# Three mixtures of experts in a perceiver network: gates by tiles, prefix sums by doubling, first gathers ahead of the second weights, statistics by four tiles, and the rounding of a layer's weights in cross attention

## The chip, the core and the metric

The kernel runs on one core of a Trainium2 chip. A core has TensorE (PE, with its weight loads as PEld), VectorE (DVE), ScalarE (ACT), GpSimd (POOL) and SyncE (SP); each takes its instructions in the order in which the program has them. The metric is the device time of one execution in microseconds (us); lower is better. Times are medians of several runs, and one further execution is recorded by the profiler.

## The reference, cut to what matters

1024 tokens of 256 numbers (16 batches of 64) go through four layers. Each layer adds to x a cross attention over a context of 1601 rows a batch, a self attention and a feed-forward part, each on a plain layer norm of x. The feed-forward parts of layers 0, 2 and 3 are mixtures of eight experts; layer 1's has two matrices whose weights are rounded to −1, 0, 1 times a scale:

```python
x = x + _L0_ffn_ref(_layernorm(x, axis=-1), L0_ffn_Wg, L0_ffn_W1, L0_ffn_W2, L0_ffn_W3)
...
# a mixture with two choices, layer 3; layer 0 has no capacity and a gated hidden layer
logits = x_flat @ router_w.T
top_v, top_i = jax.lax.top_k(jax.nn.softmax(logits, axis=-1), K)
top_v = top_v / jnp.sum(top_v, axis=-1, keepdims=True)
for k in range(K):
    pos = jnp.take_along_axis(jnp.cumsum(onehot, axis=0), eid[:, None], axis=1)[:, 0] - 1
    keep = pos < C
    ...
    h = jax.nn.gelu(jnp.einsum('ech,ehf->ecf', expert_in, w1), approximate=False)
    y = jnp.einsum('ecf,efh->ech', h, w2)
    out = out + tok * (gate * keep.astype(x.dtype))[:, None]
# layer 2: one choice, logits through a reduction to 16
logits = (x @ wg_red.T) @ wg_unit.T
```

All of it is float32. The kernel need not compute every expert for every token: it sorts tokens by expert.

## The kernel before, in words

x and its normalised copy xn lie on chip, as eight tiles of 128 tokens (NT = 8). The stages follow each other in order: layer 0's cross attention, attention, feed-forward, then layer 1's, and so on. Their times in the profiled execution, from the start of the span: layer 0's mixture 616 to 853, layer 1's cross attention 853 to 1700, its attention 1700 to 1780, its feed-forward 1780 to 1866, layer 2's mixture 2438 to 2595, layer 3's 3051 to 3273.

**A mixture** runs so. `ready` (L298) and `normalise` (L314) make xn of a tile: statistics on DVE, three small operations on POOL with the power −1/2 among them, and one ACT pass. `expert_rows` (L1580) writes xn to DRAM as one transfer (xin, the table that is gathered from) with 128 zero rows behind it, and transposes xn whole. `gate_logits` (L1423) makes the eight logits of each token, 32 matmul records in all; layer 2 goes through 16 numbers first. `top2` and `first_max` (L1405, L1388) find the choices as one-hot tiles on DVE. `places` (L1431) finds each choice's place in its expert's list: a matmul with ones gives counts by tile, one add after the other sums them up over the 16 (layer 2: 8) groups, a matmul with a triangle counts inside a tile. `slots` (L1449) turns places into a row of a tile (lo) and a tile (hi), builds V on DVE and POOL, and for each group compares a row of numbers with lo (R, 128x128) and multiplies R by V; the sums are `token` and `share` for each row of each tile. `rows` holds the expert of each tile and is ready earlier.

`experts` (L1519) then runs 23 tiles (layer 2: 15) of 128 gathered tokens. `fetch` (L1527) reads the expert's row number into a register of SP, starts the tile's weights as two transfers (W, three buffers; 1536 and 768 KB in layer 0, 1024 and 1024 in layer 3, 1024 and 1028 in layer 2) and has POOL gather the rows (xs, three buffers). PE turns xs, makes the hidden layer and the output; DVE scales it by share, and POOL adds it into a DRAM table, `total`, by an indirect transfer. Fetches run two tiles ahead. At the end x is read back in four transfers, and `ready` runs over all tiles.

```python
got = [fetch(0), fetch(1)]
xT = turn(got[0][1])
for i in range(tiles):
    W, xs = got.pop(0)
    if i + 2 < tiles:
        got.append(fetch(i + 2))
```

**Cross attention of layer 1** (L582) has 16 batches of 13 key tiles. At step t PE makes the scores of tile t (pss, two banks), ACT copies them, DVE keeps a running maximum (top); when a batch is over, `turn` (L652) transposes the maximum, DVE reduces it (nm) and makes a diagonal of it (diag), PE spreads it, and `lower` (L670) and `values` (L676) follow 14 and 16 steps behind the scores. The context's tiles come through two ring slots, ctxT (two buffers) and ctx; further weights come through the slots wst. `quant_weight` (L1754) rounds a weight matrix: a DVE reduce of 128x2048, a small matmul, one ACT and two DVE passes. It runs for w1 in this loop (batch 12), and for w2 in layer 1's attention (L1233), step n = 3; w2 is loaded into the wst slot at 1700.90. `add_bias` (L353) adds an output bias to x on POOL, tile by tile.

What sets the order: the program's order inside stretches that are marked fixed and for instructions that are pinned (L193); elsewhere a scheduler may interleave instructions of an engine. Engines wait for each other by semaphores.

Of the kernel before, what the change touches and what calls it, by code (L numbers as in the profile page):

```python
# [16 lines left out]
P = 128  # L17
# [159 lines left out]
class Net:  # L177
    def __init__(self, tc, io):
        self.tc, self.nc, self.io = tc, tc.nc, io
        self.flip = 0  # L180
        self.w1, self.quant_next, self.xscale = None, 0, {}
        self.fixed = False
# [36 lines left out]
    def load_constants(self, pool):  # L219
# [24 lines left out]
        self.ident = self.c("ident")  # L244
        self.due = None
# [67 lines left out]

    def normalise(self):  # L314
# [38 lines left out]
    def add_bias(self, i):  # L353

        for t in range(NT):
            self.nc.gpsimd.tensor_tensor(self.x[:, t, :], self.x[:, t, :], self.bv(i), ALU.add)  # L356
# [225 lines left out]
    def L1_xattn(self, w):  # L582
# [8 lines left out]
        with (  # L591
# [4 lines left out]
            with (  # L596
# [4 lines left out]
                self.add_bias(2)  # L601
# [6 lines left out]
            with (  # L608
# [125 lines left out]

                for b in range(B):
# [14 lines left out]
                if self.w1 is not None:  # L750
                    at(NKT * 12 + 9, self.quant_weight, pst, self.w1, "pst")
                fetch(0)
# [480 lines left out]
    def L1_attn(self, w):  # L1233
# [6 lines left out]
        with tc.tile_pool(name="l1a", bufs=1) as wk:  # L1240
# [32 lines left out]
            with (  # L1273
# [39 lines left out]
                for n in range(NT + 3):  # L1313
# [8 lines left out]
                    if "L1_ffn" in self.held:  # L1322
                        if n == 3:
                            self.quant_weight(psa, self.held["L1_ffn"][1], "py")
# [63 lines left out]
    def first_max(self, small, lg, tag):  # L1388
# [3 lines left out]
        m = small.tile([P, NT, 1], F32, tag=f"m{tag}", name=f"m{tag}")  # L1392
        nc.vector.tensor_reduce(m, lg, AX.X, ALU.max)
        oh = small.tile(shape, F32, tag=f"oh{tag}", name=f"oh{tag}")
# [5 lines left out]
        lo = small.tile([P, NT, 1], F32, tag=f"lo{tag}", name=f"lo{tag}")  # L1400
        nc.vector.tensor_reduce(lo, oh, AX.X, ALU.min)
        nc.vector.tensor_tensor(oh, oh, lo.to_broadcast(shape), ALU.is_equal)
        return m, oh

    def top2(self, small, lg):  # L1405

        nc = self.nc
        shape = [P, NT, E]
        m1, oh1 = self.first_max(small, lg, "a")
        lg2 = small.tile(shape, F32, tag="lg2", name="lg2")  # L1410
        nc.vector.scalar_tensor_tensor(lg2, oh1, -BIG, lg, ALU.mult, ALU.add)
        m2, oh2 = self.first_max(small, lg2, "b")
        e2 = small.tile([P, NT, 1], F32, tag="e2", name="e2")
        nc.vector.tensor_tensor(e2, m2, m1, ALU.subtract)
        nc.scalar.activation(e2, e2, AF.Exp)
        g1 = small.tile([P, NT, 1], F32, tag="g1", name="g1")
        nc.vector.tensor_scalar(g1, e2, 1.0, None, ALU.add)
        nc.vector.reciprocal(g1, g1)
        g2 = small.tile([P, NT, 1], F32, tag="g2", name="g2")
        nc.vector.tensor_tensor(g2, e2, g1, ALU.mult)  # L1420
        return oh1, g1, oh2, g2

    def gate_logits(self, small, pp, xT, w):  # L1423
        ps = self.psum(pp, [P, NT, E], "pst")
        for t in range(NT):
            self.project_N(ps[:, t, :], xT, t, w)
        lg = small.tile([P, NT, E], F32, tag="lg", name="lg")
# [935 lines left out]
```

## Time and profile before

| | us |
|---|---|
| median of 3 runs | 3266.31 |
| lowest, highest run | 3265.10, 3282.47 |
| profiled execution | 3275.31 |
| its span, first to last instruction | 3273.5 |
| granted clock of TensorE, mean | 0.953 |

The page of the profile gives busy times by engine, the span in 40 slices, DMA queues, the chain that ended last, and the costliest groups of instructions. Busy shares of the span: PE 92%, ACT 42%, DVE 39%, POOL 11%; the DMA engines moved 395 MB, 121 GB/s on the mean. Views of single stretches show each instruction as start, duration, engine, line, operation, output and inputs, and in brackets how long its engine was idle before it and what ended that. A view of windows gives the busy time of each engine, the granted clock, the DMA share and the rate in a stretch. Periods of an expert tile, from the same trace: 8.17 in layer 0, 7.24 in layer 2, 7.25 in layer 3.

### The profile page before, as it was taken

Reading aid. Unit: us, or ns where it says so; the run is one execution under the profiler, and the core shown is the slowest. Engines: PE = TensorE matmul, PEld = TensorE weight load, DVE = VectorE, ACT = ScalarE, POOL = GpSimd, SP = SyncE. Lnnn points to the kernel's source line nnn. Section 1 sums busy time; section 2 is a strip of 40 time slices with the busy share of each in tenths; the row PEclk is TensorE's granted clock in tenths of the full one; section 3 lists DMA queues with packets and bytes.
Section 4 is the critical chain, followed back from the end, with each engine's and each line's share of the span. In section 5 each row is a group of like instructions: output and inputs, shape, how many; then the busy total and the mean of one; then the engine's idle time right before and its main releaser. Section 6 shows DMA issues by size and latency. Waiting matters only on the chain. (4 is left out here: it accounts for less than half of the span.)

```text
span 3273.5 us, 67440 instructions
## 1 busy us (share of the span) xinstructions
PE 3021.5 (92%) x28567; PEld 2263.0 (69%) x28567; DVE 1261.0 (39%) x3415; ACT 1362.1 (42%) x2699; POOL 371.6 (11%) x538
## 2 busy tenths in 40 slices
PE   7999997699799999999998999999979798889798
PEld 5666664599556666666666777777748676778697
DVE  6888884422244444444446521221242100035200
ACT  5888884211233333333333522222222387763111
POOL 0000001233200000000010000000012311111232
PEclk9999998699899999999997999999988899999799
DMA  6334431389211121211257011111208555510497
GB/s 216 106 130 134 134 108 42 134 287 323 63 61 61 61 81 44 78 61 61 81 174 221 28 46 55 61 41 61 77 17 300 161 180 187 175 56 1 152 328 241
DMA packets 178362, 395.09 MB, mean 121 GB/s; under 512 B 11446, under 2 KB 142270, under 8 KB 165214
## 3 DMA queue, kind: packets, MB, share of 16 engines
q1 hardware_dynamic: 165070, 372.91, 33.0%
q0 software_dynamic: 11712, 16.00, 2.4%
q8 instruction: 225, 3.69, 0.5%
q10 hardware_dynamic: 1280, 1.88, 0.2%
q14 instruction: 75, 0.61, 0.1%
HBM read 375.02 MB, written 16.12 MB: 119 GB/s over the span
## 5 line engine op out<-in xcount | busy, mean ns | idle before, releaser
L199 PE MATMUL acc<-ctx,st 128*128 128x257 f32 (+1 forms) x1664 | 397.2, 383 | 0.0
L199 PE MATMUL pss<-qk,ctxT 128*128 128x512 f32 (+1 forms) x832 | 388.8, 592 | 0.6 <-DVE qk L634 0.6
L199 PEld LDWEIGHTS acc<-ctx,st 128*128 128x128 f32 (+1 forms) x1664 | 310.1, 190 | 94.6 <-issue 35.6
L459 DVE CUSTOM_DVE_ANT_0 Sx<-s,mneg 128x384 f32<-128x384 f32 (+1 forms) x512 | 264.2, 570 | 88.6 <-PE s L199 88.6
L650 DVE TENSOR_TENSOR top<-pss,top 128x512 f32<-128x512 f32 x192 | 132.7, 691 | 402.4 <-ACT st L645 402.3
L203 PE MATMUL pst<-cst,Sx 128*128 128x128 f32 (+1 forms) x1736 | 255.8, 286 | 25.5 <-ACT Sx L1369 10.3
L674 ACT ACTIVATE st<-st 128x512 f32<-128x512 f32 (+1 forms) x208 | 130.6, 629 | 292.5 <-DVE st L673 292.5
L935 ACT ACTIVATE Pr<-pss 128x512 f32<-128x512 f32 (+1 forms) x512 | 219.9, 523 | 62.1 <-PE pss L199 60.7
L503 ACT ACTIVATE PT<-pst 128x384 f32<-128x384 f32 x512 | 215.1, 489 | 63.4 <-PE pst L203 62.3
L203 PEld LDWEIGHTS pst<-cst,Sx 128*128 128x128 f32 (+1 forms) x1736 | 188.7, 143 | 73.1 <-ACT PT L503 27.8
L199 PEld LDWEIGHTS pss<-qk,ctxT 128*128 128x128 f32 (+1 forms) x832 | 154.1, 186 | 120.7 <-issue 102.7
L645 ACT COPY st<-pss 128x512 f32<-128x512 f32 (+1 forms) x208 | 121.8, 585 | 201.5 <-PE pss L199 201.5
L199 PE MATMUL pso<-W,hT 128*128 128x256 f32 x884 | 200.9, 379 | 0.0
L199 PE MATMUL pst<-wst,ctxT 128*128 128x256 f32 (+1 forms) x832 | 183.4, 380 | 0.0
L199 PE MATMUL psk<-ctxT,wst 128*128 128x512 f32 (+1 forms) x512 | 181.8, 513 | 0.8 <-ACT qT L797 0.8
L199 PEld LDWEIGHTS pso<-W,hT 128*128 128x128 f32 x884 | 163.2, 190 | 19.7
L199 PEld LDWEIGHTS pst<-wst,ctxT 128*128 128x128 f32 (+1 forms) x832 | 153.5, 186 | 25.9 <-issue 2.7
L199 PE MATMUL pss<-q,ctxT 32*128 32x128 f32 (+1 forms) x3328 | 149.6, 298 | 13.6 <-issue 9.5
L199 PEld LDWEIGHTS psk<-ctxT,wst 128*128 128x128 f32 x512 | 88.3, 190 | 93.7 <-issue 92.1
L356 POOL TENSOR_TENSOR x<-x,bvec 128x256 f32<-128x256 f32 x40 | 29.8, 746 | 1079.2 <-ACT xn L317 1079.2
L837 DVE TENSOR_TENSOR v<-pst,bvec 128x512 f32<-128x512 f32 (+1 forms) x112 | 73.1, 653 | 204.4 <-PE pst L199 204.4
L478 ACT ACTIVATE Sx<-Sx,neg 128x384 f32<-128x384 f32 (+1 forms) x256 | 145.8, 620 | 11.5 <-DVE neg L469 11.3
(394 smaller groups left out, 4479.5 us busy)
## 6 DMA issues: line engine op xcount, KB each, us to landing
ctxT<-in_ctxT_dram SPq DMA_DIRECT2D x64, 1601.0 KB
W<-in_L_experts_dram SPq DMA_DIRECT2D x61, 1024.0 KB
ctx<-in_ctx_dram SPq DMA_DIRECT2D x32, 1536.0 KB
W<-in_L_experts_dram SPq DMA_DIRECT2D x23, 1536.0 KB
ctx<-in_ctx_ones_dram SPq DMA_DIRECT2D x16, 1632.0 KB
ctx<-in_ctx_one_dram SPq DMA_DIRECT2D x16, 1542.0 KB
W<-in_L_experts_dram SPq DMA_DIRECT2D x23, 768.0 KB
W<-in_L_experts_dram SPq DMA_DIRECT2D x15, 1028.0 KB
```

The costliest lines, as they stand in the source:

```text
L199: self.pinned(self.nc.tensor.matmul(out, lhsT, rhs, start=start, stop=stop))
L203: self.pinned(self.nc.tensor.transpose(out, in_, self.ident[:n, :n]))
L356: self.nc.gpsimd.tensor_tensor(self.x[:, t, :], self.x[:, t, :], self.bv(i), ALU.add)
L459: self.pinned(nc.vector.tensor_tensor_reduce(out=Sx[:, j, :n], in0=ps[j][:, :n], in1=st["mneg"][:, o : o + n], op0=ALU.add, op1=ALU.max, s ...
L478: self.pinned(nc.scalar.activation(Sj[j], Sj[j], AF.Identity, bias=st["neg"][:, j - 2 : j - 1]))
L503: self.pinned(nc.scalar.activation(PT, ps, AF.Exp))
L645: pin(nc.scalar.copy(st[:kn], ps[:kn]))
L650: pin(nc.vector.tensor_tensor(top[b][:kn], ps[:kn], top[b][:kn], ALU.max))
L674: pin(nc.scalar.activation(st, st, AF.Exp, scale=HD**-0.5))
L837: nc.vector.tensor_tensor(o, ps[:kn, :n, :], bv[:kn].to_broadcast([kn, n, D]), ALU.add)
L935: nc.scalar.activation(st["Pr"][:kn, g : g + n, j, :], ps[j][:kn, :n, :], AF.Silu)
```

## The change

1. **Gates by tiles.** `expert_rows` and the old `gate_logits` go. The new `gate_logits` writes xin tile by tile (eight transfers), turns a tile with two transposes, copies it on ACT, and makes its logits with two matmuls (in layer 2 two more steps: 16 numbers, then logits); turns run one tile ahead. All of it is pinned, and two PSUM buffers serve it. The normalisation of the last tile is pinned after the fourth turn. The zero rows come from one small tile that is filled once at the start.
2. **Choices and prefix sums.** `top2` writes into the joint tiles, without the copies in `two_choices`. `places` copies the counts once and adds them to themselves shifted by 1, 2, 4 and 8 groups.
3. **R four groups wide**: 4 compares of 128x512 in place of 16 of 128x128.
4. **First gathers.** W[0] is fetched, then two gathers are started, and then POOL copies `rows` to `rest`, from which the register for W[1] and all later ones is read.
5. **Statistics by four tiles** (`ready_all`) behind the mixtures of layers 0 and 2: one power on POOL for four tiles, ACT and DVE share the normalising. The bias add of layer 1's cross attention moves from its projections to step 3 of its loop, and bias adds are pinned everywhere.
6. **w2 of layer 1** is loaded into a ctxT slot in cross attention (batch 15, step 1) and rounded there (step 7), no longer in attention. Layer 2's cross attention weights are thereby loaded earlier into wst. The last normalisation before a mixture or layer 1's feed-forward part moves into that part.

```diff
+    def ready_all(self):
+        nc, pin = self.nc, self.pinned
+        self.fixed = True
+        parts = []
+        for h in range(2):
+            mv = self.stat.tile([P, 4, 2], F32, tag="mv4", name="mv4", bufs=2)
+            for i in range(4):
+                st = self.stat.tile([P, 6], F32, tag="bst", name="bst")
+                pin(nc.vector.bn_stats(st, self.x[:, 4 * h + i, :]))
+                pin(nc.vector.bn_aggr(mv[:, i, :], st))
+            rs = self.stat.tile([P, 2, 4], F32, tag="rs4", name="rs4", bufs=2)
+            pin(nc.vector.tensor_scalar(rs[:, 0], mv[:, :, 1], 1e-5, None, ALU.add))
+            nc.gpsimd.tensor_tensor(
+                rs[:, 0], rs[:, 0], self.c("pow")[:, 0:1].to_broadcast([P, 4]), ALU.pow
+            )
+            parts.append((mv, rs))
+        for h, (mv, rs) in enumerate(parts):
+            pin(nc.vector.scalar_tensor_tensor(
+                rs[:, 1], mv[:, :, 0], -1.0, rs[:, 0], ALU.mult, ALU.mult
+            ))
+            for i in range(4):
+                o, x = self.xn[:, 4 * h + i, :], self.x[:, 4 * h + i, :]
+                if i % 2:
+                    pin(nc.vector.tensor_scalar(
+                        o, x, mv[:, i, 0:1], rs[:, 0, i : i + 1], ALU.subtract, ALU.mult
+                    ))
+                else:
+                    pin(nc.scalar.activation(
+                        o, x, AF.Identity, bias=rs[:, 1, i : i + 1], scale=rs[:, 0, i : i + 1]
+                    ))
+        self.fixed = False
...
-            self.nc.gpsimd.tensor_tensor(self.x[:, t, :], self.x[:, t, :], self.bv(i), ALU.add)
+            self.pinned(self.nc.gpsimd.tensor_tensor(
+                self.x[:, t, :], self.x[:, t, :], self.bv(i), ALU.add
+            ))
...
-                self.add_bias(2)
...
+                at(3, self.add_bias, 2)
...
+                    at(NKT * 15 + 1, self.load_w2)
+                    at(NKT * 15 + 7, lambda: self.quant_weight(pst, self.w2, "pst"))
...
-                        if n == 3:
-                            self.quant_weight(psa, self.held["L1_ffn"][1], "py")
...
-        cum = small.tile([P, G + 1, E], F32, tag="cum", name="cum")
-        nc.vector.memset(cum[:, 0, :], 0.0)
-        for g in range(G):
-            nc.vector.tensor_tensor(cum[:, g + 1, :], cum[:, g, :], ps[:, g, :], ALU.add)
-        ps = self.psum(pp, [P, G, E], "pst")
-        self.mm(ps.rearrange("p g e -> p (g e)"), self.c("tri"), flat)
+        within = self.psum(pp, [P, G, E], "pst")
+        self.mm(within.rearrange("p g e -> p (g e)"), self.c("tri"), flat)
+        cum = [small.tile([P, pad + G, E], F32, tag=f"cum{i}", name="cum") for i in range(2)]
+        for c in cum:
+            nc.vector.memset(c[:, :pad, :], 0.0)
+        nc.vector.tensor_copy(cum[0][:, pad:, :], ps)
+        step = 1
+        while step < G:
+            nc.vector.tensor_tensor(
+                cum[1][:, pad:, :], cum[0][:, pad:, :], cum[0][:, pad - step : pad - step + G, :],
+                ALU.add,
+            )
+            cum.reverse()
+            step *= 2
         place = small.tile([P, G, E], F32, tag="place", name="place")
-        nc.vector.tensor_tensor(place, ps, cum[:, :G, :], ALU.add)
-        return place, cum[:, NT, :], cum[:, G, :]
+        nc.vector.tensor_tensor(place, within, cum[0][:, pad - 1 : pad - 1 + G, :], ALU.add)
+        return place, cum[0][:, pad + NT - 1, :], cum[0][:, pad + G - 1, :]
...
-        for g in range(G):
-            R = small.tile([P, P], F32, tag="R", name="R", bufs=3)
-            nc.vector.tensor_scalar(R, self.c("iota128"), lo[:, g : g + 1], None, ALU.is_equal)
-            self.mm(ps, R, V[:, :, g, :], g == 0, g == G - 1)
+        for g in range(0, G, 4):
+            R = small.tile([P, 4, P], F32, tag="R", name="R", bufs=2)
+            nc.vector.tensor_tensor(
+                R, self.c("iota128").unsqueeze(1).to_broadcast([P, 4, P]),
+                lo[:, g : g + 4].unsqueeze(2).to_broadcast([P, 4, P]), ALU.is_equal,
+            )
+            for i in range(4):
+                self.mm(ps, R[:, i, :], V[:, :, g + i, :], g + i == 0, g + i == G - 1)
...
-        def fetch(i):
+        def fetch(i, rows):
             W = wp.tile([P, width], F32, tag="W", name="W", bufs=3)
             r = nc.values_load(
                 rows[0:1, i : i + 1], [mybir.EngineType.SP], min_val=0, max_val=(E - 1) * P
             )
             for o in (slice(0, cols), slice(cols, width)):
                 nc.sync.dma_start(W[:, o], self.io[weights][bass.ds(r, P), o])
+            return W
+        def gather(i):
             xs = sp.tile([P, D], F32, tag="xs", name="xs", bufs=3)
             nc.gpsimd.indirect_dma_start(
                 xs, None, xin, bass.IndirectOffsetOnAxis(token[:, i : i + 1], 0),
                 bounds_check=NTOK + SPARE - 1,
             )
-            return W, xs
+            return xs
...
-        got = [fetch(0), fetch(1)]
-        xT = turn(got[0][1])
+        W, xs = {0: fetch(0, rows)}, [gather(0), gather(1)]
+        rest = sp.tile([P, tiles], U32, tag="rest", name="rest", bufs=1)
+        self.pinned(nc.gpsimd.tensor_copy(rest, rows))
+        W[1] = fetch(1, rest)
+        xT = turn(xs.pop(0))
         for i in range(tiles):
-            W, xs = got.pop(0)
             if i + 2 < tiles:
-                got.append(fetch(i + 2))
-            hT = hidden(W, xT)
+                W[i + 2] = fetch(i + 2, rest)
+                xs.append(gather(i + 2))
+            hT = hidden(W[i], xT)
             if i + 1 < tiles:
-                xT = turn(got[0][1])
+                xT = turn(xs.pop(0))
             n = hT.shape[1]
-            W2 = W[:, cols : cols + n * D].rearrange("p (c n) -> p c n", n=D)
+            W2 = W.pop(i)[:, cols : cols + n * D].rearrange("p (c n) -> p c n", n=D)
...
-            for t in range(NT):
-                self.ready(t)
-    def expert_rows(self, wk, stat, pst, name):
+            self.ready_all()
...
+    def gate_logits(self, name, small, pst):
+        nc, pin = self.nc, self.pinned
+        xin = self.dram.tile([NTOK + SPARE, D], F32, tag=f"{name}i", name=f"{name}i")
+        nc.sync.dma_start(
+            xin[NTOK:, :].rearrange("p (a d) -> p a d", d=64),
+            self.zero.unsqueeze(1).to_broadcast([P, D // 64, 64]),
+        )
+        lg = small.tile([P, NT, E], F32, tag="lg", name="lg")
+        self.fixed = True
+        if name == "l2":
+            sq = small.tile([E, 16], F32, tag="sq", name="sq")
+            nc.vector.tensor_tensor(sq, self.wg2, self.wg2, ALU.mult)
+            nr = small.tile([E, 1], F32, tag="nr", name="nr")
+            nc.vector.tensor_reduce(nr, sq, AX.X, ALU.add)
+            nc.gpsimd.tensor_tensor(nr, nr, self.c("pow")[:E, 1:2], ALU.pow)
+            nc.vector.tensor_scalar(nr, nr, 1e-4, None, ALU.max)
+            nc.vector.reciprocal(nr, nr)
+            wu = small.tile([E, 16], F32, tag="wu", name="wu")
+            nc.vector.tensor_scalar(wu, self.wg2, nr, None, ALU.mult)
+            ps = self.psum(pst, [P, E], "pst")
+            self.tr(ps[:16, :], wu)
+            wuT = small.tile([16, E], F32, tag="wuT", name="wuT")
+            nc.vector.tensor_copy(wuT, ps[:16, :])
+        turned = {}
+        def turn(t):
+            nc.sync.dma_start(xin[t * P : (t + 1) * P, :], self.xn[:, t, :])
+            ps = self.psum(pst, [P, 2, P], "pst")
+            for kc in range(2):
+                self.tr(ps[:, kc, :], self.xn[:, t, kc * P : (kc + 1) * P])
+            turned[t] = small.tile([P, 2, P], F32, tag="gx", name="gx", bufs=2)
+            pin(nc.scalar.copy(turned[t], ps))
+        def logits(t):
+            xT = turned.pop(t)
+            ps = self.psum(pst, [P, P], "pst")
+            if name == "l2":
+                w = self.gates[:, :, 2 * E : 2 * E + 16]
+                for kc in range(2):
+                    self.mm(ps[:16, :], w[:, kc, :], xT[:, kc, :], kc == 0, kc == 1)
+                xr = small.tile([16, P], F32, tag="xr", name="xr", bufs=2)
+                pin(nc.vector.tensor_copy(xr, ps[:16, :]))
+                turned[t] = xr
+                return
+            o = 0 if name == "l0" else E
+            for kc in range(2):
+                self.mm(ps[:, :E], xT[:, kc, :], self.gates[:, kc, o : o + E], kc == 0, kc == 1)
+            pin(nc.vector.tensor_copy(lg[:, t, :], ps[:, :E]))
+        def reduced(t):
+            if name == "l2":
+                ps = self.psum(pst, [P, P], "pst")
+                self.mm(ps[:, :E], turned.pop(t), wuT)
+                pin(nc.vector.tensor_copy(lg[:, t, :], ps[:, :E]))
+        for t in range(NT + 2):
+            if t < NT:
+                turn(t)
+            if 0 <= t - 1 < NT:
+                logits(t - 1)
+            if 0 <= t - 2 < NT:
+                reduced(t - 2)
+            if t == 3:
+                self.normalise()
+        self.fixed = False
+        return xin, lg
...
-        oh = small.tile([P, 2 * NT, E], F32, tag="oh", name="oh")
-        nc.vector.tensor_copy(oh[:, :NT, :], oh1)
-        nc.vector.tensor_copy(oh[:, NT:, :], oh2)
-        gate = small.tile([P, 2 * NT], F32, tag="gate", name="gate")
-        nc.vector.tensor_copy(gate[:, :NT], g1[:, :, 0])
-        nc.vector.tensor_copy(gate[:, NT:], g2[:, :, 0])
...
+    def load_w2(self):
+        (self.w2,) = self.slot(self.stream, "ctxT", (self.io["L1_w2T"],))
...
             turn_x(0)
+            self.normalise()
...
+                after = stages[i + 1] if i + 1 < len(stages) else None
+                load(after)
                 getattr(self, name)(held.pop(name))
-                self.normalise()
+                if after not in ("L0_ffn", "L1_ffn", "L2_ffn", "L3_ffn"):
+                    self.normalise()
```

## The prediction, made before the changed kernel ran

> **What bounds the kernel now.** I read the page first, its share and clock rows, then the costliest groups, and then the stages one by one by the windows and the timeline.
>
> The page's first part:
>
> ```profile
> span 3273.5 us, 67440 instructions
> ## 1 busy us (share of the span) xinstructions
> PE 3021.5 (92%) x28567; PEld 2263.0 (69%) x28567; DVE 1261.0 (39%) x3415; ACT 1362.1 (42%) x2699; POOL 371.6 (11%) x538
> ```
>
> TensorE is busy 92% of the span, and the change takes hardly a matmul out of the long loops. So nothing can be won in cross attention or among the expert tiles: the windows of the loops show PE busy 90.00 of 90.00 us (740 to 830, layer 0) and 80.00 of 80.00 (3100 to 3180, layer 3). What can be won is the 8% in which PE waits, and the change works where much of it sits: ahead of each mixture, and behind two of them. The timeline of layer 0's start (start, duration, engine, line, operation, idle before and who ended it):
>
> ```profile
> 626.79 0.23 DVE L1428 COPY lg<-pst 128x64 f32<-128x64 f32 x1 [5.84 <-PE pst L199]
> 631.03 3.10 DVE L1442 TENSOR_TENSOR cum<-cum,pst 128x8 f32<-128x8 f32 x16 [0.66 <-PE pst L199]
> ...
> 637.70 4.30 SPq L1533 DMA_DIRECT2D W<-in_L_experts_dram  x6
> ...
> 642.75 5.39 PE L199 MATMUL pst<-V,R 128*128 128x69 f32 x24 [1.49 <-DVE R L1506]
> ...
> 649.17 1.30 POOL L1535 DMA_INDIRECT xs<-l0i,token  x1 [9.93 <-DMA W<-in_L_experts_dram]
> ...
> 655.86 0.66 PE L203 MATMUL pst<-cst,xs 128*128 128x128 f32 x2 [7.71 <-DMA xs<-l0i,token]
> ```
>
> One serial chain runs from the logits (626.79) to the first gathered rows (655.86): 29 us with little of PE in it. Its two long links are the prefix sums (3.10 us) and the gather, issued at 649.17 while the six weight DMAs of 637.70 still land; PE waits for it until 655.86, 6.7 us.
>
> **The change, part by part** (us; negative is faster; bounds in brackets).
>
> *1. Gates by tiles.* The windows ahead of the logits (length, PE, PEld, DVE, ACT, POOL, clock, DMA share, GB/s):
>
> ```profile
> 616.00:618.00 2.00, 0.58 (x5) 0.45 (x5) 1.54 (x4) 1.07 (x2) 0.65 (x4) 1.00 0.43 41
> 618.00:620.00 2.00, 0.65 (x6) 0.39 (x4) 0.00 (x0) 0.60 (x1) 0.92 (x3) 1.00 0.89 343
> 620.00:622.00 2.00, 1.44 (x13) 1.22 (x11) 0.69 (x1) 0.59 (x1) 0.00 (x0) 0.99 0.87 293
> 622.00:624.00 2.00, 2.00 (x11) 2.00 (x11) 0.00 (x0) 0.00 (x0) 0.00 (x0) 0.50 1.03 345
> ```
>
> 32 gate matmuls take 5.97 us, mostly at clock 0.50. In their place come eight steps of two transposes, an ACT copy, two matmuls and a small DVE copy. With two PSUM buffers a step is the round trip transposes, copy, next: at full clock 0.28 (eight transposes took 1.09 at 3051.41) + 0.37 (the 128x256 copy of 656.56) + two hand-overs of about 0.1 = 0.87; at half clock 0.69 (the pair of 2598.01) + 0.37 + 0.2 = 1.3. The order of the changed kernel puts every gate transpose behind the last matmul of the stage before, so the steps start near 617.0 in layer 0 and 3051.4 in layer 3. I take five steps at full and three at half clock, 8.2, and 0.6 for the last logits: 625.8 against 626.79, **−1.0** [−2.4, +1.4]; 3060.2 against 3061.75, **−1.5** [−2.8, +0.9]. Layer 2 has three matmul steps a tile, and its first ACT copy stands behind xn6 (done 2442.43): 8 × 1.25 + 1.5 gives 2453.9 against 2452.35, **+1.5** [−1, +4.4]. With no gate transposes between its steps, layer 0's attention loses a stall of 0.8 near 602 (PE waited 2.08 for xn): **−0.8** [−0.8, 0].
>
> [...] The rows show 1.00 from 616 to 620 with PE busy 0.58 and 0.65 of 2 us, and 0.50 only later. [...]
>
> *2. Prefix sums, copies.* 16 dependent adds (3.10) become one PSUM copy (0.28, as the 128x128 add of 634.05) and four adds of 128x128 at 0.32: 1.56, so −1.5; the oh copies save 0.4 on the chain. **−2.0** [−2.2, −1.5] in layers 0 and 3; in layer 2 eight adds (1.55) become one copy and three adds of half the width: **−0.6** [−0.8, 0].
>
> *3. Four-wide R.* 16 compares become four of 128x512 (0.69, the diag product L659). PE's matmuls behind them set the pace (32 in 7.10 us in layer 3), so the compares are hidden, and only the first is 0.41 longer. In layer 0 the 2.28 us reduce of layer 1's weight, which stopped PE 1.49 at 642.75, now stands in DVE's order ahead of the token chain's hi: +2.28 − 1.7. **+0.6** [−0.5, +2.3] and **+0.3** [0, +0.5].
>
> *4. Gathers ahead.* Only W[0] (2.3 MB) lies ahead of the gathers, and at the 380 to 469 GB/s that the DMA view shows from 640 to 652 it has landed some 7 us after 637.70, before they are issued. Over the whole trace a gather lands 2.7 us (shortest) to 4.9 (median) after issue; the first here took 6.7. I take 3.5: **−3.2** [−4, 0], and **−3.1** in layer 3 (its wait is 7.62). Layer 2's first transposes are behind the b2 matmuls (7.27 us from 2465.88), which cover the gather: 0. The added wait: W[1] waits for two gather issues and a POOL copy, about 3.3 us after the first issue, and W[2] is queued behind it on SP. In layer 0 the first half (1.5 MB, about 4.6 us) lands some 6.5 after SP issues it, near 656, needed one tile (about 8 us) after the first hidden matmul, near 658: hidden beside the first tile.
>
> *5. Statistics by four.* POOL's order sets the pace of the transition behind layer 0:
>
> ```profile
> 866.27 2.10 POOL L356 TENSOR_TENSOR x<-x,bvec 128x256 f32<-128x256 f32 x3
> 866.35 0.60 ACT L317 ACTIVATE xn<-x,rs 128x256 f32<-128x256 f32 x1 [1.10 <-POOL rs L311]
> ...
> 867.70 14.74 PE L199 MATMUL pst<-xnT,wst 128*128 128x512 f32 x30
> ```
>
> Statistics reach DVE at 853.48, yet xn7 comes at 866.35, since each tile takes three POOL operations and a bias add, 1.8 us. Now DVE's statistics (0.55 a tile, 8.2 in all with two pow of about 1.0 and four normalisings) give xn7 near 861.7; the projections, 32 × 0.49 behind the last transposes near 862.7, end at 878.4 instead of 882.4: **−4.0** [−5, −2]. Behind layer 2 there were no bias adds (xn7 at 2604.85): **−2.5** [−5, −1]. The adds go into cross attention, where POOL is idle.
>
> *6. Layer 1's w2.* In attention its rounding held DVE from 1751.98 to 1754.54, and PE waited 2.92 for A at 1755.72: **−3.0** [−3, −1]. In cross attention w1's rounding at 1500.4 to 1505.3 stopped PE nowhere. But w2 goes into the slot whose batch ends at 1612.3, and its reduce is in DVE's order between nm and diag of that turn:
>
> ```profile
> 1612.32 0.37 SPq L261 DMA_DIRECT2D ctxT<-in_ctxT_dram  x1
> ...
> 1617.06 0.68 DVE L657 TENSOR_REDUCE nm<-pst 128x4 f32<-128x512 f32 x1
> ...
> 1617.77 0.69 DVE L659 TENSOR_TENSOR diag<-cst,nm 128x512 f32<-128x512 f32 x1
> ```
>
> 1 MB issued at 1612.32 lands near 1618 (the 1.6 MB there now stopped at 1618.2); the reduce (2.29) ends at 1620.3, and behind it on DVE wait diag, the lowering and the next maximum. PE's matmul of diag, at 1619.47 now, comes near 1621.3 or later: **+2.3** [0, +6; the same load took 8.85 at 1700.90]. Layer 1's ffn starts with its normalising after the first transposes, not before its copy: **−1.4** [−1.4, 0]. Earlier weight loads and the zero rows are far ahead of their use: 0.
>
> **Sum.** Layer 0: −0.8 −1.0 −2.0 +0.6 −3.2 = −6.4. Layer 3: −1.5 −2.0 +0.3 −3.1 = −6.3. Layer 2: +1.5 −0.6 = +0.9. Transitions: −6.5. Layer 1: +2.3 −3.0 −1.4 = −2.1. Together **−20.4**. The profiled execution took 3275.31 (span 3273.5, 1.8 outside it); it would take 3254.9. It lay 9.0 above the median 3266.31 and above two of the three runs; the stages summed here are short and serial, so I carry the difference, not a ratio: 3266.3 − 20.4 = **3246**. Errors of separate terms partly cancel: the forecast's own range is 3239 to 3253.
>
> **Rivals.**
> - *Half clock in the gate loops.* All steps at 1.3, layer 2's at 1.6: 2.4 more in layers 0 and 3 each, 2.9 in layer 2, so −12.7: 3254. For it: the clock was 0.50 in 2443 to 2448. Against: the rows above.
> - *The gathers stay slow*, because their time is their own and not the weights': −6.3 is gone, 3252. For it: the longest landing in the trace is 8.1 without such a burst. Against: the median is 4.9 with DMA engines 0.93 to 0.96 busy.
> - *It does not do what it says*: compares and prefix sums hidden, gathers slow, statistics bound by the read of x: only −2.1 of layer 1 and about −3 stay: 3261.
> - *Slower: the weight stream.* The loops move 320 to 335 GB/s with the DMA engines 0.93 to 0.96 busy, and the weights alone need 2.36 MB in 8.17 us, 289 GB/s. The two early weight tiles were a lead, and the change takes it. If W then got under 289 GB/s, each of the 61 tiles would wait: a tile costs 2.36/p or 2.1/p. At p = 260 that is 0.91 × 23 + 0.82 × 23 + 0.82 × 15 = +52, net +32: 3298; the gain is gone at 277. Against it: three buffers allow only two tiles of lead anyway, and PE was busy throughout in 740 to 830.
>
> **How the numbers follow.** Forecast 0.58, half clock 0.15, slow gathers 0.12, not as said 0.06, slower 0.09. The range goes down to the sum of all lower bounds (−35, 3231) and up over the first three rivals (to 3261) to no gain at all, 3266; all upper bounds at once (+8, 3275) would need every term to fail. A measurement tells 0.5%, 16.3 us, from no change: faster lies under 3250, which three quarters of the forecast and a little of the rivals reach, 0.47; slower 0.09; within, 0.44.
>
> **What would show it.** Gates: the time from the last matmul before to lg, and the clock of those windows. Prefix: four adds of 0.3 in place of 3.10. Gathers: first xs at PE under 4 us after issue, with no PE wait for W in the first three tiles. Transition: xn7 under 862.5 − 853.5 = 9 us after the first statistics. w2: PE's idle time ahead of diag's matmul in that turn; no 2.92 in layer 1's attention. Wrong if tile periods (8.17, 7.24, 7.25) grow, or diag's matmul waits 8 us.

## The result, and the profile after

| us | before | changed |
|---|---|---|
| median of 20 runs each | 3277.48 | 3269.26 |
| lowest, highest run | 3265.10, 3287.73 | 3258.65, 3278.36 |
| profiled execution | 3275.31 | 3261.79 |
| its span | 3273.5 | 3259.6 |

The ratio is 0.9974, 95% interval [0.9964, 0.9983]: 8.5 us faster. That is clear of the scatter, and less than the 0.5% that the prediction asked of a change to call it faster. The forecast, 20.4 less, has the right sign and 2.4 times the size. Its absolute number, 3246, missed by more, since it started from the median of three runs, 3266.31; twenty runs put that kernel at 3277.48, near the profiled 3275.31 that the sum was made on.

The changed kernel's page: TensorE's busy time is as before (3021.5), and the span 13.9 shorter.

```profile
span 3259.6 us, 67485 instructions
## 1 busy us (share of the span) xinstructions
PE 3022.1 (93%) x28591; PEld 2267.8 (70%) x28591; DVE 1263.2 (39%) x3391; ACT 1361.4 (42%) x2709; POOL 358.9 (11%) x495
```

Layer 0's start in its timeline (start, duration, engine, line, operation, idle before and who ended it):

```profile
628.67 0.17 DVE L1680 COPY lg<-pst 128x8 f32<-128x8 f32 x1 [1.18 <-PE pst L199]
...
632.94 1.27 DVE L1479 TENSOR_TENSOR cum<-cum 128x128 f32<-128x128 f32 x4
...
650.16 1.31 POOL L1582 DMA_INDIRECT xs<-l0i,token  x1 [8.44 <-DVE share L1560]
...
653.34 0.66 PE L203 MATMUL pst<-cst,xs 128*128 128x128 f32 x2 [4.19 <-DMA xs<-l0i,token]
```

The prefix sums (3.10 before) and the first gather (6.7 from issue to PE, now 3.2) shrank as forecast. But the logits are complete at 628.84, not at 625.8. The windows ahead of them (length, PE, PEld, DVE, ACT, POOL, clock, DMA share, GB/s) show what happened: the loop got one step of 0.87 and one of 1.28, and from the third on, at half clock, each took 1.60.

```profile
616.00:618.00 2.00, 1.36 (x8) 0.96 (x7) 1.01 (x5) 0.78 (x3) 1.01 (x3) 1.00 0.31 76
618.00:620.00 2.00, 1.87 (x13) 1.50 (x13) 0.47 (x3) 0.72 (x3) 1.01 (x3) 0.95 0.85 206
620.00:622.00 2.00, 1.74 (x9) 1.65 (x9) 0.17 (x1) 0.94 (x3) 0.00 (x0) 0.50 0.73 280
622.00:624.00 2.00, 1.74 (x9) 1.64 (x8) 0.17 (x1) 0.67 (x2) 0.00 (x0) 0.50 0.98 318
```

The statistics behind layer 0 do what was forecast. The last normalising, now DVE's, ends at 859.38, where xn7's began at 866.35, and the same projections end at 875.25 (timeline):

```profile
857.74 1.64 DVE L341 TENSOR_SCALAR xn<-x,mv,rs 128x256 f32<-128x256 f32 x2
...
860.55 14.70 PE L199 MATMUL pst<-xnT,wst 128*128 128x512 f32 x32
```

Layer 1's w2 reaches its slot, and its reduce stands between nm and diag; PE waits 1.69 (timeline):

```profile
1608.17 0.37 SPq L263 DMA_DIRECT2D ctxT<-in_L_w2T_dram  x1
...
1614.14 2.29 DVE L1840 TENSOR_REDUCE wa<-ctxT 128x1 f32<-128x2048 f32 x1 [0.55 <-DMA ctxT<-in_L_w2T_dram]
1616.34 0.68 DVE L696 TENSOR_TENSOR diag<-cst,nm 128x512 f32<-128x512 f32 x1
1617.17 1.10 PE L199 MATMUL pst<-diag,cst 128*128 128x512 f32 x2 [1.69 <-DVE diag L696]
```

In return layer 1's attention lost its stall, and more with it. Before, PE's wait of 2.92 in front of 1755.72 was followed by 16 us at half clock, with PE busy all the time; windows of the kernel before, then of the changed one:

```profile
1752.00:1756.00 4.00, 1.07 (x34) 0.96 (x32) 3.96 (x4) 0.70 (x2) 0.00 (x0) 0.90 1.09 333
1756.00:1760.00 4.00, 4.00 (x38) 3.15 (x38) 2.82 (x7) 0.60 (x1) 1.01 (x3) 0.50 1.11 336
1760.00:1764.00 4.00, 4.00 (x66) 3.75 (x65) 2.29 (x10) 0.97 (x2) 1.01 (x3) 0.50 1.10 336
```

```profile
1752.00:1756.00 4.00, 4.00 (x75) 3.44 (x74) 3.71 (x11) 1.46 (x3) 1.01 (x3) 1.00 1.11 349
1756.00:1760.00 4.00, 4.00 (x85) 3.40 (x85) 3.72 (x11) 1.62 (x4) 1.01 (x3) 1.00 1.08 330
```

The x counts tell it: 38 matmul records in 4 us before, 85 now, though both rows of 1756 to 1760 say "busy 4.00". Period of a tile: 6.2 before, 3.4 now; from the first scores to the feed-forward part's transposes 47.05 before, 36.61 now.

**Where the gain went** shows in layer 2's gates, from the last addition to x up to the first maximum: 14.95 before, 20.78 now. Timeline of the changed kernel:

```profile
2429.25 0.60 ACT L353 ACTIVATE xn<-x,rs 128x256 f32<-128x256 f32 x1 [0.54 <-POOL rs L313]
...
2429.76 0.63 ACT L1664 COPY gx<-pst 128x256 f32<-128x256 f32 x2
...
2430.16 1.04 PE L199 MATMUL pst<-gx,gates 128*16 128x128 f32 x4 [3.24 <-ACT gx L1664]
...
2433.24 0.69 PE L203 MATMUL pst<-cst,xn 128*128 128x128 f32 x2
...
2433.86 1.04 PE L199 MATMUL pst<-gx,gates 128*16 128x128 f32 x4
...
2434.82 0.59 PE L199 MATMUL pst<-wuT,xr 16*128 16x8 f32 x2
...
2435.34 0.69 PE L203 MATMUL pst<-cst,xn 128*128 128x128 f32 x2
```

Two things are to be seen. The first copy waits on ACT behind seven normalisings, and PE for it 3.24. Then a step takes 2.11 (2433.24 to 2435.34, and so on to the end), and it is PE's own work: 0.69, 1.04 and 0.59 one behind the other (their ends overlap a little), no idle time.

### The profile page after: what moved, and what is told of

Same layout as the page of the kernel before. It is cut to its first block, busy times and chain, and to the rows that moved or that the text cites. A ratio compares the mean times of both kernels' runs of the same rounds, so it can differ in the third digit from the quotient of the medians.

```text
span 3259.6 us, 67485 instructions
## 1 busy us (share of the span) xinstructions
PE 3022.1 (93%) x28591; PEld 2267.8 (70%) x28591; DVE 1263.2 (39%) x3391; ACT 1361.4 (42%) x2709; POOL 358.9 (11%) x495
## 4 chain that ended last, share of the span: by engine, by line
PE 78%; DMA 6%; DVE 5%; issue 5%; ACT 3%; POOL 2%; POOLq 0%; SPq 0%; DVEq 0%; ACTq 0%
PE acc L199 17%; PE pss L199 15%; PE pst L199 14%; PE pst L203 7%; PE psk L199 6%; PE pso L199 5%; DMA l3o<-y,token 4%; PE p L199 4%; PE s L199 3%; PE ps L199 3%; PE psh L199 2%; DMA ctx<-in_ctx_dram 1%; PE po L199 1%; ACT mneg L467 1%; ACT PT L541 1%
## 5 line engine op out<-in xcount | busy, mean ns | idle before, releaser
L516 ACT ACTIVATE Sx<-Sx,neg 128x384 f32<-128x384 f32 (+1 forms) x256 | 145.8, 621 | 11.5 <-DVE neg L507 11.3
L199 PEld LDWEIGHTS psh<-xT,W 128*128 128x128 f32 x1216 | 146.4, 197 | 3.6 <-DVE xT L191 0.9
```

The lines of the kernel that those rows point to most:

```text
L199: self.pinned(self.nc.tensor.matmul(out, lhsT, rhs, start=start, stop=stop))
L516: self.pinned(nc.scalar.activation(Sj[j], Sj[j], AF.Identity, bias=st["neg"][:, j - 2 : j - 1]))
```

## The experiments

The question was which part ate the missing 12 us, and by what. One theory: the gate loops, slower than the whole-matrix form that they replace. The rival: the loops are as forecast, and the loss lies in added waits elsewhere or in the clock of unchanged stages. Later runs ask why the gate loops are slow: a wait on ACT's order, the ring of two PSUM buffers, or the clock. Each expectation says what the theories make of its own run. Ratios are to the kernel before, with 95% intervals.

**e1_old_gates.** The changed kernel with the old gates in all three mixtures.

```diff
-            xin, lg = self.gate_logits("l0", small, pst)
+            xin, xnT = self.expert_rows(wk, stat, pst, "l0")
+            lg = self.gate_logits(small, pst, xnT, self.gates[:, :, 0:E])
```

> The changed kernel with the whole-matrix gate logits of before (one write of xn, all transposes, 32 gate matmuls in a row; everything else of the change is kept). Theory A, gates by tiles lost what the rest gained, since transposes that lay beside the stage before now lie on the path and the steps run at clock 0.50: from the last residual add to the last logits 10.5 to 11 us again in layers 0 and 3 and 14.5 in layer 2, against 11.9, 12.5 and 20.6 in the changed kernel, so some 8 us less than the changed kernel, 16 less than before (ratio to before near 0.995). Theory B, as predicted: the gates cost about the same either way, ratio to before 0.997 as for the changed kernel.

Measured: 3261.41 us, 0.9948 [0.9933, 0.9962], where the changed kernel has 0.9974: the gates by tiles cost some 8.5, give or take 6. Layer 2's gates are back at 14.92. Without part 1 the prediction's sum is −18.6; the ratio says −17.0 [−22, −12]. So the first theory holds. That the rest of the sum comes out about right is in part luck: in the trace of the changed kernel, layer 1's attention gave 7.4 more than forecast, and the clock took 2.7 back at the start of layer 1's scores.

**e2_w2_in_cross_attention, e3_gathers_ahead, e4_statistics.** The kernel before with part 6, part 4 or part 5 alone. The edits are those parts of the diff:

```diff
# e2
+                    at(NKT * 15 + 1, self.load_w2)
+                    at(NKT * 15 + 7, lambda: self.quant_weight(pst, self.w2, "pst"))
# e3
+        W, xs = {0: fetch(0, rows)}, [gather(0), gather(1)]
# e4
-                self.add_bias(2)
+                at(3, self.add_bias, 2)
-            for t in range(NT):
-                self.ready(t)
+            self.ready_all()
```

> The kernel before, with only the load and the rounding of layer 1's w2 moved into cross attention. Theory A, the stall of 2.92 us in layer 1's attention also made the clock fall to 0.50 for the next 15 us and again at the start of layer 1's feed-forward part: attention and the start of the feed-forward part are 9 to 11 us shorter in the trace (tiles at 3.4 us in place of 6.2, clock 1.00 from 1752 on), cross attention 2 longer, 7 to 9 less in all. Theory B, as predicted: only the stall goes, 3 less and 2 more, 1 less in all.

> The kernel before, with only the first gathers ahead of the second weights. Theory A, the burst of weights made the first gather slow: first rows at PE 3.2 us after the issue in layers 0 and 3 in place of 6.7, 7 us less in all, no PE wait for weights in the first tiles. Theory B, a first gather takes 6 to 7 us by itself: no change.

> The kernel before, with only the statistics by four tiles behind the mixtures of layers 0 and 2 and the bias adds in the loop. Theory A, as in the two traces: 4.8 less up to the end of the projections behind layer 0's mixture, 4.0 less behind layer 2's, some of it lost to a stretch of half clock at the start of the scores (2.7 in the trace of the changed kernel): 5 to 9 less. Theory B, the transition is set by the read of x and the time comes back as waits for the context: under 2 less.

Measured: e2 3273.07, 0.9984 [0.9973, 0.9996], so −5.2 [−8.8, −1.3] against −0.7 forecast for what it holds (+2.3 −3.0; part 6's normalising is not in e2). Its trace has layer 1's attention at 36.47, 10.6 less, and the start of layer 1's feed-forward part 2.7 less; it gives 1.5 back at diag, 4.0 from the rest of that part to the end of layer 2's attention and 6.7 in layer 3's cross attention and attention. e3 3271.62, 0.9981 [0.997, 0.9992], −6.2 against −6.3; gather to PE 3.24 and 3.14 where it was 6.69 and 6.62. e4 3274.01, 0.9989 [0.9975, 1.0003], −3.6 against −6.5, with zero inside the interval; its trace shows −4.7 and −1.8 at the two transitions, the forecast's size, and +2.8 between the first scores of layer 1 and batch 14's diag, where no instruction was changed but the bias adds.

**e5_layer2_whole.** The changed kernel, old gates in layer 2 only.

```diff
-            xin, lg = self.gate_logits("l2", small, pst)
+            xin, xnT = self.expert_rows(wk, stat, pst, "l2")
...
+            lg = self.whole_logits(small, pst, xr, wuT)
```

> The changed kernel with the whole-matrix gate logits in layer 2 alone; layers 0 and 3 keep their gates by tiles. Theory A, nearly all that the gates lost lies in layer 2 (20.8 us from the last residual add to the first maximum in place of 15.0; layers 0 and 3 lie within 1.4 of before): that stretch is 15 us again, and the kernel 6 us under the changed one, ratio to before near 0.9955. Theory B, the loss is spread over the three mixtures: half of that or less.

Measured: 3255.92, 0.9935 [0.9918, 0.9952]; layer 2's gates 14.86. It is no slower than e1, so layer 2's loop is the one that costs; the forms in layers 0 and 3 can't be told apart by total times.

**e6_own_banks.** The changed kernel with the logits in PSUM banks that lie idle then (the expert tiles' own), not in the two that the transposes use.

```diff
-            ps = self.psum(pst, [P, P], "pst")
+            ps = self.psum(pl, [P, D], "pso")
```

> The changed kernel with PSUM banks of their own for the logits (and for layer 2's second product), so that the turns have both of the two old ones. Theory A, the two banks chain the steps, and a step at half clock falls from 2.11 us to about 1.6 in layer 2 and from 1.60 to about 1.55 in layers 0 and 3 (PE's own 0.69 + 0.86 at that clock): 4 us less in layer 2, under 1 elsewhere. Theory B, PE's own work at half clock is the step (0.69 + 1.04 + 0.59 in layer 2): no step changes by more than 0.1.

Measured: 3255.93 in a single run. Layer 0's gates fell to 7.12 from 11.91: a step is 0.70 on the mean, and the clock lasts until 623.8, when the loop is all but over. Its windows:

```profile
620.00:622.00 2.00, 2.00 (x19) 1.73 (x18) 0.50 (x3) 1.51 (x5) 0.12 (x1) 1.00 0.89 336
622.00:624.00 2.00, 2.00 (x17) 1.77 (x16) 0.50 (x3) 0.90 (x3) 0.00 (x0) 0.95 0.93 301
624.00:626.00 2.00, 0.50 (x3) 0.41 (x2) 1.28 (x6) 0.00 (x0) 0.00 (x0) 0.50 0.98 252
```

In the changed kernel the first two windows had nine records and 0.50. Layer 3's gates took 9.27 (12.49 with the shared ring). The traces of e10 and e11, which have these banks too, repeat it: layer 0's gates took 7.12 to 7.17 in three traces with own banks and 11.5 to 11.9 in four with the shared ring, layer 3's 8.6 to 9.3 and 11.9 to 12.5. In layer 2 nothing changed, 20.78, as a loop without PE idle time can gain nothing from a bank. So the ring is the cause in layers 0 and 3, and not in layer 2.

**e9_layer2_interleaved.** The changed kernel, but in layer 2 ACT normalises tile t just before tile t's copy, and not all of them first.

```diff
+        late, self.later = self.later, None
         for t in range(NT + 2):
+            if late and t < NT:
+                self.due = late[t]
+                self.normalise()
             if t < NT:
```

> The changed kernel, with layer 2's normalisings put between the turns on ACT: xn of a tile, then that tile's turned copy, and so on, in place of seven normalisings ahead of the first copy. Theory A, layer 2 lost because the first copy stood behind xn6: PE idles 3.2 us, the clock falls to 0.50, and eight steps of 2.11 us follow one after the other; with the steps spread over the normalising (one tile in 1.14 us) most of the loop lies beside it, and from the last residual add to the first maximum it takes 9 to 12 us in place of 20.8 (before: 14.95); the kernel is 9 to 11 us under the changed one, ratio to before near 0.994. Theory B, the steps are too short of work to hold the clock up anyway: half clock from the start, eight steps of 2.11 from the last residual add on, 17 to 18 us, 3 us gained.

Measured: 3268.41, 0.9969 [0.9956, 0.9982], not to be told from the changed kernel. Layer 2's gates took 18.13: the idle 3.24 is gone, 2.65 of it is won, and the rest of the loss stays. Its windows:

```profile
2426.00:2430.00 4.00, 4.00 (x17) 2.37 (x16) 0.89 (x4) 1.53 (x5) 0.24 (x1) 0.50 0.19 66
2430.00:2434.00 4.00, 4.00 (x17) 2.43 (x16) 0.89 (x4) 1.53 (x5) 0.00 (x0) 0.50 0.19 66
2434.00:2438.00 4.00, 4.00 (x18) 2.18 (x15) 0.89 (x4) 0.81 (x2) 0.00 (x0) 0.50 0.11 37
```

12 us of PE without a gap, and the clock doesn't come back. In e1 the old form meets half clock in the same place, and it does:

```profile
2426.00:2430.00 4.00, 2.89 (x8) 1.30 (x9) 0.85 (x2) 1.71 (x4) 0.46 (x2) 0.50 0.48 161
2430.00:2434.00 4.00, 4.00 (x8) 0.74 (x6) 0.68 (x1) 0.00 (x0) 0.00 (x0) 0.76 0.31 101
2434.00:2438.00 4.00, 2.39 (x20) 2.21 (x20) 2.42 (x10) 0.26 (x1) 0.00 (x0) 1.00 0.02 4
```

What runs there differs: eight records with 512 moving columns in e1; records with 128 and 8 columns, and transposes, in e9. Which of this decides the traces don't show.

**e7_reduce_later, e8_warm.** e7 is e1 with the reduces of w1 and w2 pinned to turns where DVE is free. e8 adds to e7 four matmuls that nobody reads, behind the keys at the start of layer 1's scores.

```diff
# e7
-                    at(NKT * 15 + 7, lambda: self.quant_weight(pst, self.w2, "pst"))
+                    at(NKT * 15 + 5, lambda: sums.update(w2=self.quant_sum(self.w2)))
+                    at(NKT * 15 + 8, lambda: self.quant_weight(pst, self.w2, "pst", sums["w2"]))
# e8
                     keys(0, j)
+                    warm = self.psum(pss, [P, 512], "pss")
+                    self.mm(warm[:, :256], self.c("ones"), qT[:, 0, :256])
```

> The kernel with the old gates and the rest of the change (e1), with the two reduces of the weight rounding pinned to later steps of cross attention (w1: batch 12, step 6; w2: batch 15, step 5). Theory A, the wait for w2's landing and its reduce ahead of diag cost 1.7 us of PE: PE's wait ahead of diag's matmul is gone and the cross attention 1.5 to 2 shorter than in e1; nothing new stalls. Theory B, the 2.29 us reduce delays PE wherever it stands in the loop: no change. Against e1 some 2 us less, near 0.9943 of before.

> e7 with four further matmuls of 128x256 whose result nobody reads, one behind each of the first four key products of layer 1's cross attention, in the gaps that PE has there. Theory A, the gaps of that stretch (PE busy 1.3 to 1.6 of 2 us) let the clock fall to 0.50 for 6 us at the start of the scores whenever the projections start early: with them filled it stays at 1.00, and from the end of the projections to the diagonal of batch 14 it takes 2.5 less than in e1 and e7 (less the 0.5 to 1 that the matmuls themselves add). Theory B, the fall has another cause: the clock falls as before and the matmuls add 0.5 to 1.9.

Measured: e7 3252.52, 0.9925 [0.9906, 0.9943]; first scores to diag 734.73 where e1 had 736.42, so the wait of 1.7 at diag is gone. e8 3255.34, 0.9936 [0.992, 0.9953]; first scores to diag 731.94, the other 2.8. The windows of the changed kernel and then of e8 show it, a dip to half clock behind some us of PE three quarters busy, and none where the gaps are filled:

```profile
878.00:882.00 4.00, 3.03 (x17) 2.00 (x15) 0.85 (x2) 0.74 (x2) 0.00 (x0) 0.65 0.00 0
882.00:886.00 4.00, 4.00 (x6) 1.48 (x5) 0.63 (x1) 0.59 (x1) 0.00 (x0) 0.50 0.01 2
```

```profile
878.00:882.00 4.00, 4.00 (x11) 1.60 (x9) 1.93 (x3) 1.20 (x3) 0.00 (x0) 1.00 0.01 2
882.00:886.00 4.00, 4.00 (x11) 1.80 (x10) 1.53 (x3) 1.18 (x3) 0.00 (x0) 1.00 0.02 4
```

The 2.8 is shown in its place, but not in the whole: e8's time is not below e7's.

**e10_all, e11_best.** e10 is the changed kernel with the edits of e6, e7, e8 and e9. e11 is e5 (layer 2 whole) with own banks for the logits of layers 0 and 3, and the edits of e7 and e8.

> The changed kernel with four of the edits tried here together: logits in PSUM banks of their own, layer 2's normalisings between its turns, the reduces of the weight rounding at later steps, the four filling matmuls at the start of layer 1's scores. If the stretches add up: layer 2's gates 9 to 12 us below the changed kernel's, cross attention 1.7 and 2.8 shorter, the logits of layers 0 and 3 1 to 4 shorter; 15 us under the changed kernel, ratio to before 0.990 to 0.993, below e7's 0.9925. If the clock takes back what the stretches give, as it did with e8 against e7: 0.9925 to 0.995.

> The combination of the edits tried here without the one that fell short: whole-matrix gate logits in layer 2 (e5), logits in banks of their own in layers 0 and 3 (e6), the reduces at later steps (e7), the four filling matmuls (e8). If the stretches add up: 3 us under e10 (layer 2's gates 14.9 in place of 18.1), ratio to before 0.9905 to 0.992. Rival, the clock's own scatter hides 3 us: anywhere between 0.9905 and 0.9935.

Measured: 3250.98, 0.9919 [0.9906, 0.9932], and 3251.15, 0.9922 [0.9905, 0.994]. Both beat both kernels, and so do e1, e5, e7 and e8; e10, e11 and e7 can't be told apart. The gates of layers 0, 2 and 3 took 7.15, 18.08, 8.72 in e10 and 7.17, 14.91, 8.55 in e11.

**e12_changed_again.** The changed kernel as it is, once more.

> The changed kernel itself once more, for the scatter of stretches whose code is the same. Theory A, the granted clock of the stretches made of short steps is not fixed by the program: layer 3's cross attention and attention (443.6 us in the changed kernel's first trace, 443.8 to 455.5 in the others) and layer 3's gates (12.5) come out otherwise by several us, while layer 2's gates (20.8), the gathers (3.2, 3.1) and layer 1's attention (36.6) are the same within 0.3. Theory B, each kernel has its own fixed clock pattern: all stretches within 1 us of the first trace.

Measured: 3269.34, span 3267.3, where the first profile had 3259.6. The stages that the change touched repeat: gates 11.91, 20.73, 12.46 (first 11.91, 20.78, 12.49), layer 1's attention 36.70. Of the 7.7 us between the spans, 6.6 lie in one stage with the same code: layer 3's cross attention and attention took 450.20, after 443.61. Of these, 5.4 are idle time of PE for which the profile names no releaser ("issue": 25.0 in all, after 19.6).

**The clock beside TensorE's busy time.** The 52 clock records in the trace of the changed kernel, and the 52 of the kernel before, hold 0.50 and 1.00 only; other values in a window are means over it. PE's busy time in the records does not sort the windows: 4.00 of 4 us stand at 0.50 in e9 (2430 to 2434) and at 1.00 in e8 (878 to 882), and 0.65 of 2 at 1.00 in the kernel before (618 to 620). What ran in them differs in the number of records and in their columns; no run was made to tell which of it the clock follows.

Transposes alone stood ahead of one rise. Behind layer 2's mixture of the changed kernel, sixteen of them follow 12.89 us of idle time, and the clock goes from 0.50 to 1.00 at 2596.1, before any other matmul (timeline, then windows):

```profile
2591.88 3.74 PE L203 MATMUL pst<-cst,xn 128*128 128x128 f32 x16 [12.89 <-ACT xn L345]
2596.56 1.39 PE L199 MATMUL pss<-q,ctxT 32*128 32x128 f32 x38 [0.94 <-POOL q L955]
```

```profile
2594.00:2596.00 2.00, 1.62 (x8) 1.22 (x6) 1.03 (x2) 0.77 (x2) 1.69 (x2) 0.50 0.00 0
2596.00:2598.00 2.00, 1.39 (x38) 1.23 (x38) 0.35 (x1) 0.25 (x1) 0.35 (x1) 0.97 0.04 8
```

## Why the prediction was wrong, point by point

**The step that failed: part 1, gates by tiles, layer 2's "+1.5 [−1, +4.4]" above all.** It measured +5.8, beyond its upper bound; layer 3's −1.5 measured +1.4; layer 0's −1.0 measured +1.0, its −0.8 in attention can't be seen (the last addition to x comes between 613.4 and 619.1 over the traces). The old form varies too, 10.7 to 12.1 in layer 0 and 8.4 to 11.5 in layer 3 over seven traces, so that only layer 2's loss stands far outside of it. Forecast −1.8 in all, measured +8.2 in the stages (+8.5 against the old form's means) and +8.5 by e1: 10 of the missing 12 us. The working went wrong in two places.

- *The length of a step.* Layer 2's step was taken as 1.25, like a round trip between PE and ACT. It is 2.11, the sum of what PE does in it at half clock. I summed only hand-overs and never PE's own work. (The sum for layer 0's step, 0.28 + 0.37 + 0.2, is 0.85 and not 0.87, and the first rival's five slower steps cost 2.2 and not 2.4; neither matters.) The old form needs 8 records of 512 columns for the 16 numbers; the new one 32 of 128, at 1.04 for four, 8.3 in all.
- *The clock.* I read 1.00 from 616 to 620, with PE busy a third of the time, as a sign that the loop would hold it for five steps. It did not last in that trace either: the drop came at 621.9. In layers 0 and 3 the ring of two buffers left PE waiting for the copy of the logits, 0.26 in each loop step at half clock, and such a step took 1.60 (1.3 assumed). In layer 0 of the changed kernel the clock fell at 619.8, by the third loop step; in e6 it fell at 623.8, and the loop was nearly over by then. From 616 to 620 PE was busy 3.23 of 4 us in the changed kernel and 2.78 in e6, so busy time up to the drop doesn't tell them apart. Without the ring, too, the loop doesn't hold the clock: e6's drop came behind two windows with PE busy 2.00 of 2.00. In layer 2 of the changed kernel the clock fell at 2428.9, ahead of the first logits, and stayed at 0.50 until 2473.2, past the end of the loop. In e9 it stayed there with PE busy 4.00 of 4 for 12 us; in e1, with the wide records, it was back at 1.00. Why it comes back for the one and not for the other is not shown.

The first rival, half clock in the gate loops, had the clock right, at a chance of 0.15. Its price in layer 2, 1.6 a step, was too small as well. That the loops hold transposes does not by itself account for it: sixteen of them were all that PE ran in the 16 us ahead of the rise at 2596.1.

**Part 2.** −2.0 twice measured −1.55 and −1.62 (the copies saved nothing beside the sums); layer 2's −0.6 measured −0.1 up to place and −0.3 behind it.

**Part 3.** +0.6 and +0.3 measured +0.7 and +0.4, right, and by the mechanism told: where the reduce of layer 1's weight is moved away (e7, e8, e10, e11), layer 0's stretch is 1.3 shorter than before, so that the reduce costs 2.1.

**Part 4.** −3.2 and −3.1 measured −3.5 and −3.55, and −6.2 alone (e3): right, the gather had waited for the weights. The slow-gather rival falls. So does the slower one: the expert tiles of layer 0 take 190.4 from the first turn to the last output, as before (190.2).

**Part 5.** −4.0 and −2.5 measured −4.8 and −1.8: both inside their bounds, and right in sum by errors that cancel. Unforeseen was the clock behind it: +2.8 at the start of layer 1's scores in e4, and, with part 6's wait of 1.7 on top, 3.9 to 4.8 in the changed kernel's two traces, e1, e5 and e6 (2.0 for both in e9); with the filling matmuls (e8, e10, e11) it is gone. PE's busy time doesn't explain the dip: before, PE was busy 2.85 and 3.39 of 4 us from 882 to 890, at 1.00. Nor does the code: e9 has the changed kernel's there and lost only 0.3 beside the wait of 1.7. What sets it off is not shown.

**Part 6.** w2's reduce: +2.3 measured +1.7, the mechanism as told. The feed-forward part's start: −1.4 measured −1.5. Layer 1's attention: −3.0 [−3, −1] measured −10.4, a second wrong size, on the good side. I priced the stall at its own length; it also put the 16 us behind it at half clock, until 1772.2 (e2, with the stall gone, took 10.6 less). The stage spent 30.7 us at half clock before and 13.7 now. That price varies: in e4, whose attention is the old one, it spent 27.3 so and took 42.99.

**What is left open.** The first two profiles differ by −13.9, the medians by −8.2. Code that the change left alone scatters: layer 3's cross attention and attention took 443.8 to 450.5 in four traces of the kernel before and of single parts (before, e2, e3, e4), and 443.6 to 459.1 in the ten others, on the mean 447 and 451. Whether the change costs some 4 us there, or the clock and the "issue" idle time (19.6 to 27.3) vary by chance or from chip to chip (the runs used several), these runs don't tell. The prediction's range had no term for it.

## What to carry to other kernels

Price a short stage by both the hand-overs and the sum of TensorE's own work, at the clock that the stage before leaves behind, and don't count on a high clock in a nearly idle window (here 1.00 with PE busy 0.65 of 2 us, and 0.50 from 621.9 on). Busy time is no guess at the clock either: 4.00 of 4 us stood at 0.50 in e9 and at 1.00 in e8. Cutting a matrix product into tiles to start earlier trades wide matmuls for many narrow ones; here it paid in layer 0, with PSUM banks of their own for the pieces (7.12, the old form 10.7 to 12.1), and not where it quadrupled the records (20.78, the old form 14.95). The stall of 2.92 us ahead of a stretch of small matmuls went with 10.4 us, over three times its length, so look at the clock behind a stall before pricing it.

## What the runs showed of the hardware

- TensorE busy in the records did not by itself bring the clock back. It stayed at 0.50 through 12 us of 4.00 of 4 (e9, layer 2), while with eight records of 512 columns in the same place it was 1.00 within 8 us (e1: 0.50, 0.76, 1.00 in three windows of 4). In layer 1's attention before, with matmuls of 34, 64 and 256 columns, it stayed at 0.50 for 16 us with PE busy 4.00 of 4, and came back at 1772.2.
- Sixteen transposes were all that TensorE ran in the 16 us before its clock went from 0.50 to 1.00 (the changed kernel, 2596.1).
- The same program took 3259.6 and 3267.3 of span, 6.6 us of it in one stage, so a change's worth of under 8 us is read from its own stage in the trace, or from some 20 runs, not from two spans.
